# A two-layer graph attention kernel: a buffer of its own for the last products of W with a_dst, and the transposes of tile 4 ahead of two mask counts

## The chip, the cores and the metric

The kernel runs on one core of a Trainium2 chip. The core has five engines that work in parallel, each through its own queue in order: TensorE (PE; its weight loads are shown apart as PEld), VectorE (DVE), ScalarE (ACT), GpSimd (POOL) and SyncE (SP, which here only issues DMAs). The metric is the device time of one execution in microseconds; several executions are made, and their median is compared.

## The reference, cut to what matters

Two graph attention layers on 3327 nodes of 1024 features, each followed by a residual and a layer norm. The adjacency is an int32 matrix in which about one entry in 200 is set.

```python
def _L0_gnn_ref(x, adj, W, a_src, a_dst):        # H = 8 heads of 128
    h = (x @ W).reshape(C, H, D)
    h_heads = jnp.transpose(h, (1, 0, 2))
    alpha_src = jnp.einsum('hcd,hd->hc', h_heads, a_src)
    alpha_dst = jnp.einsum('hcd,hd->hc', h_heads, a_dst)
    e = alpha_src[:, :, None] + alpha_dst[:, None, :]
    e = jnp.where(e >= 0, e, NEG_SLOPE * e)
    e = jnp.where(adj[None] == 0, -jnp.inf, e)
    attn = jax.nn.softmax(e, axis=-1)
    out = jnp.einsum('hij,hjd->hid', attn, h_heads)
    return jnp.transpose(out, (1, 0, 2)).reshape(C, H * D)
...
x = _layernorm(x + _L0_gnn_ref(x, adj, L0_gnn_W, L0_gnn_a_src, L0_gnn_a_dst), axis=-1)
x = _layernorm(x + _L1_gnn_ref(x, adj, L1_gnn_W, L1_gnn_a1, L1_gnn_a2), axis=-1)
```

Layer 1 is the same with one head, its own W and vectors, and a ReLU on the result.

## The kernel before

The nodes are cut into NT = 26 tiles of 128 rows. There are three stages in time: the projection with the making of edge lists (to about 487 us of the span), the sparse sums of layer 0 (gathers of rows of h0_d), and those of layer 1 with its projection (gathers of rows of y_d). A dense arm stands behind a branch and isn't taken here. The change is in the first stage, where the order of the work on every engine is written out by hand: each engine does its part in the order in which the code names it.

What the first stage does for a tile t:

- `load_x(t)` brings the rows of x (tag "x", 3 buffers); `flip(t)` transposes them: 8 transposes on PE (L176) in two groups of four, each into a PSUM bank of tag "T" (2 buffers), and two copies on ACT (L179) into xT (3 buffers). The small matmuls of the counts use the tag "T" too.
- `project(t, c)` multiplies xT by the columns `CUTS0[c]` to `CUTS0[c+1]` of wt (L479, 8 steps; two records each in the trace) into an accumulator of tag "A" (2 buffers); `keep(t, c)` copies it out with ACT (L496, and for c = 2 L491 to L494) and, after the third, stores the tile.
- wt is W with 16 columns added at its right end: W times a_src and a_dst by heads. Chunk c = 2 holds them, so `project(t, 2)` needs them all.
- `score_column(k)` makes these columns for the k-th block of 128 rows of W. DVE multiplies by a_src out of PSUM (pr0, L579) and reduces (L580). For k < 6 POOL multiplies by a_dst (pr1, L576) and ACT sums it in eight pieces (L585). For k of 6 and 7 DVE does the second product too (L579 into pr1) and reduces it (L582). pr0 and pr1 have two buffers each.
- `count(t)` is the count of the mask's rows: POOL clears the diagonal (L308), ACT sums the 3328 bytes of each row (L311) and casts the sum (deg_b, L313), DVE packs the mask (L318); then `load_mask(t + 3)` issues the DMA of a later mask from POOL (L468).
- `Edges.ends` and `ends2` make running sums of the counts: a small matmul each (L327, L346), a copy on ACT (L328, L347), then small operations on POOL (L335 to L353). `factors` has four more on POOL (L296 to L299) behind ACT's L295.
- `listing()` is a generator of steps: DVE finds the set columns (`keys`, `columns`), `places` makes a matrix with ACT (L384, L385) and DVE (L391, L392), and PE sorts the lists with it (`give`: L411, L401), which ACT and DVE take out (`take`: L423 to L428, `sources`: L436 to L450). `pace()` calls the next steps after every second k of a paced `project`. The first call in `project(2, 2)` makes three steps: `count(3)`, `places` of tile 0, and the first `give`.

Between `score_column(7)` and `count(0)` the code makes constants of the lists with DVE and POOL by turns (`tri`, `edge_constants`, L615 to L630). DVE has these behind its last product.

Of the kernel before, what the change touches and what calls it, by code (L numbers as in the profile page):

```python
# [19 lines left out]
P = 128  # L20
# [6 lines left out]
def kernel(  # L27
# [29 lines left out]
    N, D = x.shape  # L57
# [76 lines left out]
    def load_rows(dst, src, t):  # L134

        n = rows(t)
        if n < P:
            nc.gpsimd.memset(dst, 0.0)
        for r in pieces(t):
            nc.sync.dma_start(dst[r], src[at(t, r), :])  # L140
# [312 lines left out]
    with ExitStack() as own, tc.manual_schedule():  # L453
        ph = Phase(own, "proj", {"A": 2, "S": 1, "T": 2})
# [4 lines left out]
        def load_x(t):  # L459
            if t < NT:  # L460
                xts[t] = ph.sbuf("x", [P, D], 3)
                load_rows(xts[t], x, t)

        def load_mask(t):
            if t < NT:
                ads[t] = masks[t % 4 if t < NT - 1 else 4]
                for r in pieces(t):
                    nc.gpsimd.dma_start(ads[t][r, :N], adj[at(t, r), :])  # L468

        def flip(t):  # L470
            xT[t] = ph.sbuf("xT", [P, KT, P], 3)
            for _ in ph.transposed(xT[t], xts.pop(t), (0, 1)):
                pass

        def project(t, c, paced=True):

            acc = accs[t, c] = bank("A", [P, CUTS0[c + 1] - CUTS0[c]], "mm")
            for k in range(KT):
                nc.tensor.matmul(  # L479
                    acc, xT[t][:, k, :], wt[:, k, CUTS0[c] : CUTS0[c + 1]], start=k == 0, stop=k == KT - 1  # L480
                )
                if paced and k % 2 == 1:
                    pace()
# [17 lines left out]
        def count(t):  # L501
            if t < NT:
                lists[t].words(ads.pop(t), junk)
                load_mask(t + 3)
# [63 lines left out]
        junk = pool.tile([P, NP], U8, bufs=1, name="junk")  # L568
        junk_h = pool.tile([P, DH], BF16, bufs=1, name="junk_h")
        def score_column(k):  # L570
            pr = [ph.sbuf(f"pr{n}", [P, D], 2) for n in range(2)]
            to = [wt[:, k, D + n * H : D + (n + 1) * H] for n in range(2)]
            heads = [pr[n].rearrange("p (h d) -> p h d", h=H) for n in range(2)]
            for n in range(2):
                if n and k < 6:
                    nc.gpsimd.tensor_tensor(pr[n], wt[:, k, :D], av, OP.mult)  # L576
                else:
                    a = avs[:, 2 * n : 2 * n + 2, :].rearrange("p a b -> p (a b)")
                    nc.vector.tensor_tensor(pr[n], wt[:, k, :D], a, OP.mult)  # L579
            nc.vector.tensor_reduce(to[0], heads[0], AX.X, OP.add)  # L580
            if k > 5:
                nc.vector.tensor_reduce(to[1], heads[1], AX.X, OP.add)  # L582
                return
            for h in range(H):
                nc.scalar.activation(junk_h, heads[1][:, h, :], AF.Copy, accum_out=to[1][:, h : h + 1])  # L585

        flip(0)
        score_column(0)
        score_column(1)
        load_mask(0)  # L590
        project(0, 0, False)
        keep(0, 0)
        flip(1)
        load_x(3)
        score_column(2)
        project(0, 1, False)
        keep(0, 1)
# [45 lines left out]
        keep(1, 2)  # L643
        lists[0].ends2(all_b)
        lists[1].ends(tri_b)
        count(2)
        flip(3)
        load_x(5)

        done[0], slots[:] = 4, [9, (NT - 3) * 12 + 13]  # L650
        project(2, 2)
        keep(2, 2)
        lists[1].ends2(all_b)
        lists[2].ends(tri_b)
        flip(4)
        project(3, 2)
        keep(3, 2)
        lists[2].ends2(all_b)
        for t in range(3, NT):
# [3 lines left out]
            if t == 12:  # L663
                n, own = NT - 1, pool.tile([P, NT], I32, bufs=1, name="own")
# [565 lines left out]
```

## Time and profile before

| what | value |
|---|---|
| median of 3 runs | 1908.4 us (1906.88 to 1909.48) |
| the profiled execution | 1904.2 us, span 1902.5 us |
| PE busy | 1502.7 us, 79% of the span |
| DVE busy | 1146.0 us, 60% |
| POOL busy | 1032.3 us, 54% |
| ACT busy | 546.5 us, 29% |
| mean granted TensorE clock | 0.914 |
| data moved by DMA | 567.76 MB, mean 298 GB/s |

The span is the time from the first to the last instruction of the profiled execution; 1.7 us of its time lie outside. A busy share is an average over stages that have different limits, so the table says little of the first 90 us; for these the profile has the timeline of each engine, with the idle time ahead of an instruction and what ended it, the list of who waited for whom, and the busy time by stretches. In such lines the engine comes first, then the line of the code, the operation, and the tile written and read. A wait for several semaphores is put down to the one that came last.

### The profile page before, as it was taken

What the parts mean: (1) busy time and instruction counts of PE and PEld (TensorE: products, weight loads), DVE (VectorE), ACT (ScalarE), POOL (GpSimd) and SP (SyncE); (2) the same over time, 40 slices, a digit from 0 to 9 for tenths busy, and PEclk for the clock granted to TensorE, in tenths of its full rate; (3) what the DMA queues carried; (4) which work ended last, traced back from release to release, by engine and by line L of the source; (5) the groups of instructions that cost most, each with busy time, mean ns of one, the idle gap of its engine ahead of it and who ended that gap; (6) DMA issues with size and microseconds to landing.
All of it is one profiled execution on the core that took longest, in us unless ns stands there. A gap on an engine that the chain in (4) does not pass through costs nothing.

```text
span 1902.5 us, 38082 instructions
## 1 busy us (share of the span) xinstructions
PE 1502.7 (79%) x14663; PEld 887.9 (47%) x14663; DVE 1146.0 (60%) x3058; ACT 546.5 (29%) x1422; POOL 1032.3 (54%) x1391
## 2 busy tenths in 40 slices
PE   8699999999366556555556555399999999999997
PEld 5355555566254545445445444144444444444443
DVE  5799999987286666666666666344444444444442
ACT  5554544452123222222222222012222212222220
POOL 3322222220477666676666764577766667666650
PEclk9899999999678788888888888699999999999999
DMA  7656555421799999999999997899999999999980
GB/s 182 88 115 131 111 104 106 87 72 39 276 369 400 400 401 399 376 406 398 390 388 392 398 383 279 325 401 407 403 370 385 380 378 373 354 372 373 365 326 33
DMA packets 171068, 567.76 MB, mean 298 GB/s; under 512 B 27690, under 2 KB 34346, under 8 KB 170878
## 3 DMA queue, kind: packets, MB, share of 16 engines
q0 software_dynamic: 131056, 455.68, 67.2%
q1 hardware_dynamic: 39822, 109.56, 15.3%
q8 instruction: 118, 1.93, 0.4%
q14 instruction: 72, 0.59, 0.1%
HBM read 578.85 MB, written 42.97 MB: 327 GB/s over the span
## 4 chain that ended last, share of the span: by engine, by line
PE 50%; DMA 24%; DVE 12%; ACT 6%; issue 4%; POOL 3%; DVEq 0%; ACTq 0%; SPq 0%; POOLq 0%
DMA src<-h_d,idx 22%; PE mm L1023 20%; PE acc L991 12%; PE mm L479 11%; DVE e L868 3%; ACT junk L311 3%; PE acc L896 2%; PE tr L176 2%; POOL src L801 2%; DVE pr L929 1%; ACT xT L179 1%; DMA wt<-in_L_gnn_W_dram 1%; PE acc L880 1%; DVE top L274 1%; PE xp L411 1%
## 5 line engine op out<-in xcount | busy, mean ns | idle before, releaser
L801 POOL DMA_INDIRECT src<-h_d,idx x416 | 443.3, 1066 | 201.6 <-PE acc L896 52.3
L801 POOL DMA_INDIRECT src<-y_d,idx x416 | 415.4, 999 | 222.1 <-PE acc L991 89.4
L896 PE MATMUL acc<-src,e 128*32 128x128 f32 x6656 | 267.7, 328 | 260.0 <-DVE e L868 259.6
L479 PE MATMUL mm<-wt,xT 128*128 128x347 f32 (+1 forms) x1248 | 402.5, 468 | 3.1 <-DMA wt<-in_L_gnn_W_dram 2.5
L1023 PE MATMUL mm<-wt,xT 128*128 128x512 f32 x832 | 383.3, 604 | 0.8 <-DVE o L1026 0.8
L896 PEld LDWEIGHTS acc<-src,e 128*32 128x32 f32 x6656 | 226.3, 133 | 316.7 <-DVE e L868 290.7
L479 PEld LDWEIGHTS mm<-wt,xT 128*128 128x128 f32 x1248 | 228.2, 192 | 111.2 <-ACT ht L496 6.7
L1023 PEld LDWEIGHTS mm<-wt,xT 128*128 128x128 f32 x832 | 152.2, 190 | 199.5 <-issue 179.1
L991 PE MATMUL acc<-src,es 128*32 128x342 f32 (+1 forms) x2496 | 205.6, 463 | 33.8 <-DVE es L982 30.9
L868 DVE TENSOR_TENSOR e<-oh,way 128x1024 f32<-128x1024 f32 x130 | 158.8, 1221 | 60.6 <-ACT w L866 60.3
L991 PEld LDWEIGHTS acc<-src,es 128*32 128x32 f32 x2496 | 71.5, 111 | 158.8 <-issue 113.1
L866 ACT ACTIVATE w<-way 128x32 f32<-128x32 f32 (+1 forms) x130 | 24.7, 190 | 399.7 <-DVE way L864 388.3
L1026 DVE SCALAR_TENSOR_TENSOR o<-mm,y 128x512 f32<-128x512 f32 x52 | 36.0, 692 | 166.1 <-PE mm L1023 166.1
L1005 ACT ACTIVATE z<-y,ri 128x342 f32<-128x342 f32 (+1 forms) x78 | 39.5, 569 | 313.8 <-DVE ri L1001 313.8
L863 DVE TENSOR_TENSOR way<-src,re 128x32 f32<-128x32 f32 x104 | 20.9, 201 | 171.6 <-DMA src<-h_d,idx 153.2
L179 ACT ACTIVATE xT<-tr 128x512 f32<-128x512 f32 x104 | 59.3, 595 | 150.7 <-PE tr L176 150.7
L979 DVE TENSOR_TENSOR way<-way,src 128x128 f32<-128x128 f32 x104 | 31.1, 299 | 89.9 <-DMA src<-y_d,idx 44.4
L311 ACT ACTIVATE junk<-ad 128x3328 uint8<-128x3328 uint8 x26 | 78.3, 3013 | 16.1 <-POOL ad L308 16.1
L848 ACT ACTIVATE own<-own,es 128x128 f32<-128x128 f32 x208 | 63.6, 388 | 59.7 <-DVE es L845 59.7
L880 PE MATMUL acc<-end,e 128*128 128x128 f32 x416 | 63.0, 313 | 15.3 <-DVE e L868 15.3
L335 POOL TENSOR_TENSOR place_of<-cnt 128x1 f32<-128x1 f32 x26 | 5.0, 191 | 122.1 <-ACT cnt L328 102.5
L296 POOL CAST mvs<-r 128x8 bf16<-128x8 f32 x26 | 6.0, 231 | 118.2 <-ACT r L295 118.2
(188 smaller groups left out, 1953.7 us busy)
## 6 DMA issues: line engine op xcount, KB each, us to landing
h_d<-ht SPq DMA_DIRECT2D x26, 520.0 KB
own<-h_d SPq DMA_DIRECT2D x26, 520.0 KB
y_d<-y SPq DMA_DIRECT2D x26, 514.0 KB
y<-y_d SPq DMA_DIRECT2D x26, 514.0 KB
x<-in_x_dram SPq DMA_DIRECT2D x25, 512.0 KB
y<-in_x_dram SPq DMA_DIRECT2D x25, 512.0 KB
out_dram<-o SPq DMA_DIRECT2D x25, 512.0 KB
ad<-in_adj_dram POOLq DMA_DIRECT2D x25, 415.9 KB
```

Of the source, the lines that this page charges most:

```text
L176: nc.tensor.transpose(tr[:, k, :], src[:, (4 * g + k) * P : (4 * g + k + 1) * P], ident)
L179: nc.scalar.activation(part, tr, AF.Copy)
L311: nc.scalar.activation(junk, ad, AF.Copy, accum_out=self.deg)
L479: nc.tensor.matmul(acc, xT[t][:, k, :], wt[:, k, CUTS0[c] : CUTS0[c + 1]], start=k == 0, stop=k == KT - 1)
L801: nc.gpsimd.indirect_dma_start(out=s[:, g, :w], out_offset=None, in_=table[:, :], in_offset=bass.IndirectOffsetOnAxis(ap=idx[:, t, b * NG ...
L848: nc.scalar.activation(hn, hn, AF.Copy, scale=es[:, n : n + 1])
L868: nc.vector.tensor_tensor(e, oh.unsqueeze(2).to_broadcast([P, ng, H, wide]), wp.unsqueeze(3).to_broadcast([P, ng, H, wide]), OP.mult,)
L880: nc.tensor.matmul(self.acc[h // 4][:, h % 4, :], e[:, 0, h, :], rowsof[:, 0, h, :], start=False, stop=h % 4 == 3,)
L896: nc.tensor.matmul(self.acc[h // 4][g * GT : (g + 1) * GT, h % 4, :], e[:, g, h, :], rowsof[:, g, h, :], start=first and h % 4 == 0, stop= ...
L991: nc.tensor.matmul(self.acc[c][to, :m], es[:, g, :], s[:, g, CUTS[c] : CUTS[c + 1]], start=b == 0, stop=b == EB,)
L1005: nc.scalar.activation(z[:, cut], self.res[:, cut], AF.Copy, scale=ri[:, 1:2])
L1023: nc.tensor.matmul(acc, xT[:, k, :], wt1[:, k, half], start=k == 0, stop=k == KT - 1)
```

## The change

The second product of DVE, for k of 6 and 7, goes into a tile of its own, pr2, with one buffer; pr1 is left to POOL and ACT. And `flip(4)` is named right behind `load_x(5)`, ahead of `count(2)`, which itself goes behind `flip(3)` and `load_x(5)`. Before, the order was `count(2)`, `flip(3)`, `load_x(5)`, and `flip(4)` came only after `project(2, 2)` with the counts that follow it.

```diff
         def score_column(k):
-            pr = [ph.sbuf(f"pr{n}", [P, D], 2) for n in range(2)]
+
+            tags = ("pr0", "pr1" if k < 6 else "pr2")
+            pr = [ph.sbuf(tag, [P, D], 1 if tag == "pr2" else 2) for tag in tags]
...
         keep(1, 2)
         lists[0].ends2(all_b)
         lists[1].ends(tri_b)
-        count(2)
         flip(3)
         load_x(5)
+        flip(4)
+        count(2)
 
         done[0], slots[:] = 4, [9, (NT - 3) * 12 + 13]
         project(2, 2)
         keep(2, 2)
         lists[1].ends2(all_b)
         lists[2].ends(tri_b)
-        flip(4)
         project(3, 2)
```

In the queues this means: on PE the 8 transposes of tile 4 stand behind those of tile 3, ahead of `project(2, 2)`; on ACT the four copies L179 of tiles 3 and 4 stand ahead of `count(2)`. The orders on DVE, POOL and SP are unchanged.

## The prediction

> **What bounds the kernel now.** I read the per-stage table first, then the list of waits of the first 450 us, then the timeline around those waits. The edited code lies in the first 90 us of the first stage. In the table each row has a stretch, its length, then busy us and instruction counts of PE, PEld, DVE, ACT and POOL, the granted clock, the DMA share and GB/s.
>
> ```profile
> 40.00:50.00 10.00, 10.00 (x35) 6.43 (x34) 8.22 (x14) 3.18 (x15) 2.26 (x11) 1.00 0.12 12
> 50.00:60.00 10.00, 4.77 (x15) 2.85 (x14) 8.21 (x50) 4.43 (x10) 2.88 (x19) 0.76 0.43 37
> 60.00:70.00 10.00, 7.45 (x28) 4.55 (x27) 7.49 (x22) 4.74 (x11) 5.54 (x26) 0.90 0.91 169
> 70.00:80.00 10.00, 1.82 (x15) 1.31 (x16) 4.63 (x14) 7.83 (x10) 0.94 (x3) 0.62 0.98 125
> 100.00:200.00 100.00, 96.99 (x672) 59.71 (x672) 91.67 (x259) 48.13 (x134) 26.11 (x122) 1.00 0.58 126
> ```
>
> From 100 us on PE (97%) and DVE (92%) are both full: whatever starts them sooner moves all that follows. Between 50 and 80 us PE is busy only 14 of 30 us, so time is to be had there. Who is waited for:
>
> ```profile
> PE xp L411 <- DVE place L391: 20.6, 15, 9.7
> DVE pr L579 <- ACT junk_h L585: 11.0, 1, 11.0
> PE op L327 <- ACT deg_b L313: 5.0, 1, 5.0
> ```
>
> These are total, times and longest. In order of time (start, duration, engine, line, operation, idle time before it in brackets):
>
> ```profile
> 38.51 1.22 DVE L579 TENSOR_TENSOR pr<-wt,avs 128x1024 f32<-128x1024 f32 x1 [11.02 <-ACT junk_h L585]
> ...
> 54.77 2.98 ACT L311 ACTIVATE junk<-ad 128x3328 uint8<-128x3328 uint8 x1 [10.52 <-POOL ad L308]
> ...
> 58.13 0.16 PE L327 MATMUL op<-deg_b,tri_b 128*128 128x1 bf16 x1 [5.05 <-ACT deg_b L313]
> 58.48 6.69 PE L479 MATMUL mm<-wt,xT 128*128 128x346 f32 x16 [0.19 <-ACT ht L496]
> ...
> 69.52 2.98 ACT L311 ACTIVATE junk<-ad 128x3328 uint8<-128x3328 uint8 x1 [3.31 <-POOL ad L308]
> ...
> 72.73 1.07 ACT L179 ACTIVATE xT<-tr 128x512 f32<-128x512 f32 x2
> 73.69 2.98 ACT L311 ACTIVATE junk<-ad 128x3328 uint8<-128x3328 uint8 x1
> 76.89 0.71 ACT L384 ACTIVATE away<-io_q,place_of 128x512 f32<-128x512 f32 x1
> ...
> 78.18 0.26 PE L411 MATMUL xp<-mvs,place 32*128 32x42 bf16 x12 [9.71 <-DVE place L391]
> ...
> 85.50 1.09 PE L176 MATMUL tr<-ident,x 128*128 128x128 f32 x8 [0.74 <-ACT cnt L328]
> ```
>
> So: DVE sits 11.02 us in front of the second product of k = 6, whose buffer ACT still reads for k = 4. Everything on DVE behind it (the edge constants) is late, so POOL's mask edit L308 and ACT's count L311 of tile 0 are late, and ACT's copy that frees PE's accumulator stands behind that count. Later ACT does count 2, two copies of flip 3, count 3, and only then L384, for which DVE and PE wait.
>
> [...] (L576 takes 2.35 to 2.39 us beside DVE work and without). [...] after 5.05 us idle, product (1,2) took 6.69 us, against 4.71 (18.84 us for 64 records, so for 16) in the run from 34.24.
>
> **Part 1, the buffer.** Instruction counts don't change; the wait of the product of k = 6 on ACT and POOL goes. That of k = 7 still waits for DVE's own reduction of k = 6, which is ahead in its queue: free. POOL and ACT keep pr1 for k up to 5. From 38.51 to the end of the last reduction at 46.50 is 7.99 us of unbroken DVE work. It now follows the product that starts at 26.28 and takes 1.2 us: 27.5 + 8.0 = 35.5, so 11.0 sooner. W and the vectors have landed (22.4).
>
> What is late next, by copying the old distances:
> - From 46.50 to L308's end takes 8.27 us, so L308 could end at 43.8. POOL's queue ahead of it (products to 35.2, the mask issue to 35.7) is clear; mask 0 landed long before (the DMA queues are empty at 32 to 35). ACT's copy at 43.79 lasts to 44.25: count 0 runs 44.3 to 47.5 with its deg_b.
> - ACT's copy of (2,1) then waits for PE (48.4), not PE for it. PE runs (0,2) to 53.1 as before and goes straight into (1,2), warm: 53.2 to 57.9.
> - Now (0,2) is the bound. ACT's L491 moves from 58.32 to 53.2, 5.12 sooner. From there L295, POOL's eleven small operations and L308 lead to count 1: 61.58 - 5.12 = 56.46. It ends with deg_b at 59.6. In the old run ACT then waited for PE ((1,2) ended at 65.17); now it need not, so L491 of tile 1 moves from 65.20 to 59.7: 5.5 sooner.
> - POOL's chain from there to L308 of mask 2 is unbroken (65.69 to 69.49), so count 2 moves from 69.52 to 64.0.
> Part 1 is 5.5 us.
>
> **Part 2, flip 4 ahead.** Nothing is added: 8 transposes and 2 ACT copies move. On PE they pass project (2,2) with its list steps and two count matmuls; on ACT the two copies of flip 4 go from behind counts 2 and 3, L384 and tile 2's copies to before count 2, and those of flip 3 pass count 2. SP's order is the same (load_x(5) stays behind the tile-1 store; x of tile 4 was issued at 24.22, its queue is quiet by 32). POOL's and DVE's orders are the same: masks 5 and 6 are issued 5.5 or more sooner.
> - Cost on ACT: copies of flip 3 start 0.7 after the transposes, which start at 66.21 - 5.5 = 60.7: 61.4 to 62.5. The two PSUM banks of tag T are freed in turn, so flip 4's transposes run at 62.0 and 62.6 and its copies end at 63.9. Count 2 cannot start before 64.0: the old 3.31 us of ACT idle hides all four. If PE is cold there (half clock), the copies end near 65.0 and cost up to 1.0. I take 0.1.
> - Gain: between counts 2 and 3 the copies leave ACT's way: 73.69 - 72.73 = 0.96. L384 moves by 5.5 + 0.96 - 0.1 = 6.4, and with it L391 and PE's L411 (78.18 to 71.8).
> - At the old place PE loses 0.74 of wait and about 0.93 to 1.1 of transposes: project (3,2) starts 86.43 - 84.59 = 1.84 sooner. Not all counts: ACT's count 4 at 91.51 could move 1.85, but POOL ends L308 of mask 4 at 89.86 in an unbroken chain from 84.98; so 1.6. DVE has 1.83 us idle in front of L391 at 96.34, so it follows.
> Part 2 is 0.86 + 1.6 = 2.5.
>
> Masks: 3 is issued at 43.8 instead of 54.68 into an empty DMA (mask 2 alone took 36 to 42), 4 at 56.4 instead of 61.49; needed at 64.3 and 83. [...]
>
> **Sum.** 5.5 + 2.5 = 8.0 us. After 96.9 the order on every engine is as before, so the rest shifts whole; in the gather stages the DMA is at 0.99 to 1.02 of its share and starts 8 sooner. The profiled execution took 1904.2 (span 1902.5): 1896.2. The median of the runs, 1908.4, lies 4.2 above that; I take the same difference off it: 1900.4. Bounds: 7.0 if flip 4 delays count 2, 8.3 if POOL is no brake at mask 4; runs spread by 2.6.
>
> **Rivals.**
> - Only the buffer pays: flip 4 runs cold, and the 1.84 at its old place is eaten by the ACT or POOL chain. For: POOL's chain there is unbroken. Gain 4.5 to 5.5, time 1903.4. Chance 0.12.
> - Part 1 is hidden, because something besides the buffer holds count 0 or count 1 (a mask landing late, or POOL's queue), and only part 2's 2.5 is left: 1905.9, which is no change within 0.2% (3.8 us, about what a measurement tells). Against: the DMA queues are empty at 32 to 35 us. Chance 0.09.
> - Slower: the granted TensorE clock of the later stages falls. Place: from about 1240 us to the end PE is 97% busy (97.25 of 100 in 1500 to 1600, clock 1.00). Price: 660 us by 0.97, 6.4 us for each per cent of clock; 1.25% eats the gain, 1.9% makes it slower by over 0.2%. For: the layer-0 stage already shows 0.75 to 0.84. Against: 1,100 us lie between, and the work there is the same. At 2.5% it costs 16: 1916. Chance 0.05.
> - The layout does not do what it says: the product of k = 6 still waits. The wait there is on the shared buffer alone, so I leave this within the second rival.
>
> **Numbers.** Forecast 0.74, rivals 0.12, 0.09, 0.05. Faster by over 0.2%: 0.74 + 0.12 = 0.86; same 0.09; slower 0.05. Both first cases with half the spread on each side give 1898.2 to 1904.8, which leaves out some 2 in 10.
>
> **What would show it.** L579's 11.02 wait gone and the last reduction near 35.5; count 0 near 44.3 and no 5.05 idle on PE at L327; count 1 near 56.5, count 2 near 64.0, four copies ahead of it by then; the wait before L411 still long, but ending near 71.8; the L411 of 96.88 at 88.8 or so; from there equal distances. I am wrong if count 2 starts well after POOL's L308, if a mask lands late, or if the end of the first stage (486 us) does not move by about 8.

## The result and the profile after

| | median of 4 runs | span of the profiled execution |
|---|---|---|
| before | 1907.64 us (1906.47 to 1909.48) | 1902.5 us |
| changed | 1901.98 us (1900.15 to 1903.19) | 1901.5 us |

The ratio is 0.9969, with a 95% interval of 0.9951 to 0.9986: 5.7 us off the median, with 2.7 to 9.3 inside the interval. The forecast was 8.0. The two profiled spans differ by 1.0 us only: the profiled execution of before (1904.2 us) was faster than all four of its timed runs, that of the changed kernel (1903.19) was the slowest of its four. So the profile of the changed kernel has to be read by where its time lies, not by its end.

From L571 on, line numbers of the changed kernel are two higher. Its timeline, from the views of DVE, ACT and PE (start, duration, engine, line, operation, idle time before in brackets):

```profile
34.15 1.21 DVE L584 TENSOR_REDUCE wt<-pr 128x8 f32<-128x1024 f32 x1
...
46.03 2.97 ACT L311 ACTIVATE junk<-ad 128x3328 uint8<-128x3328 uint8 x1
...
54.83 4.90 PE L479 MATMUL mm<-wt,xT 128*128 128x346 f32 x16
...
61.62 0.16 PE L327 MATMUL op<-deg_b,tri_b 128*128 128x1 bf16 x1 [1.89 <-ACT deg_b L313]
...
64.50 1.08 ACT L179 ACTIVATE xT<-tr 128x512 f32<-128x512 f32 x2 [0.26 <-PE tr L176]
65.77 2.98 ACT L311 ACTIVATE junk<-ad 128x3328 uint8<-128x3328 uint8 x1 [0.19 <-POOL ad L308]
...
68.98 2.96 ACT L311 ACTIVATE junk<-ad 128x3328 uint8<-128x3328 uint8 x1
...
72.17 0.71 ACT L384 ACTIVATE away<-io_q,place_of 128x512 f32<-128x512 f32 x1
...
73.46 0.27 PE L411 MATMUL xp<-mvs,place 32*128 32x42 bf16 x12 [7.34 <-DVE place L391]
```

The 11.02 us wait of DVE is gone, and its last reduction ends at 35.36 instead of 46.51. Count 0 no longer has 10.5 us of idle before it. PE goes from (0,2) into (1,2) without a gap and at full clock (granted 1.00 over these 4.90 us): before, the same product took 6.69 us at a mean granted clock of 0.73. Count 2 starts as soon as POOL lets it (0.19 us), with all four copies done ahead of it, and count 3 follows it directly. The list of waits of the first 450 us shows the same, with one wait that has grown (DVE's in front of `tri_b`, 0.40 us before):

```profile
PE xp L411 <- DVE place L391: 18.0, 14, 7.3
...
DVE tri_b L624 <- POOL tri L620: 1.9, 1, 1.9
PE op L327 <- ACT deg_b L313: 1.9, 1, 1.9
```

DVE is now early enough to wait for POOL's last product (k = 5, 34.70 to 37.08 us), which stands ahead of the constants in POOL's queue. The table by stretches (length; busy us and counts of PE, PEld, DVE, ACT, POOL; clock; DMA share; GB/s) has PE busy 9.7 of 10 us between 50 and 60, where it had 4.8:

```profile
20.00:30.00 10.00, 7.34 (x24) 4.94 (x25) 9.89 (x10) 5.94 (x25) 4.46 (x4) 0.83 0.91 146
...
50.00:60.00 10.00, 9.73 (x36) 6.14 (x35) 3.23 (x10) 3.12 (x8) 2.85 (x13) 1.00 0.33 69
```

The row from 20 to 30 shows what went against this run: a clock of 0.83 there, where the earlier profile had 1.00. W's last block, for which PE waits there, was hardly later (before, then changed):

```profile
22.46 0.85 PE L479 MATMUL mm<-wt,xT 128*128 128x347 f32 x2 [2.46 <-DMA wt<-in_L_gnn_W_dram]
22.66 0.85 PE L479 MATMUL mm<-wt,xT 128*128 128x347 f32 x2 [2.91 <-DMA wt<-in_L_gnn_W_dram]
```

But from 24.05 to 27.47 us PE had half clock in the changed kernel (granted 0.50) and full clock before (1.00): its next 32 records took 11.04 us, before 9.51. So ACT's copy of (2,0) starts at 45.67 instead of 43.79, and in what follows I count from that copy to the first gather (before, then changed):

```profile
43.79 0.46 ACT L496 ACTIVATE ht<-mm 128x347 f32<-128x347 f32 x1 [0.88 <-PE mm L479]
488.52 1.15 POOL L801 DMA_INDIRECT src<-h_d,idx  x1 [0.96 <-issue]
...
45.67 0.46 ACT L496 ACTIVATE ht<-mm 128x347 f32<-128x347 f32 x1 [0.88 <-PE mm L479]
482.35 1.15 POOL L803 DMA_INDIRECT src<-h_d,idx  x1 [0.96 <-issue]
```

In the table all but the first column are such distances; the two L384 are those of the place matrices of tiles 0 and 1.

| start, us | copy of (2,0) | count 1, after it | count 2 | L384 | second L384 | first gather |
|---|---|---|---|---|---|---|
| before | 43.79 | 17.79 | 25.73 | 33.10 | 51.78 | 444.73 |
| changed | 45.67 | 12.59 | 20.10 | 26.50 | 43.91 | 436.68 |

The first gather, where the first stage ends, is 8.05 us sooner by this count (6.17 on the clock: 488.52 and 482.35). The rest of the difference lies later: from the first gather to the first residual copy of layer 1 (L1005) it is 746.2 us before and 751.3 after, and from there to the end 667.7 and 667.8. Whether those 5 us of layer 0 belong to the change is one question for the experiments.

The count from this copy leaves something out: DVE's moved products run from about 27 to 35 us, ahead of it. The traces of all the experiments below tell whether they hold up PE there. From PE's first matmul on W's last block to the copy of (2,0) it is 21.33 us in the first profile of before, in which the granted clock is 1.00 all through this stretch; 22.88 to 23.01 in six profiles with one drop of 3.41 us (before again, the order alone, the changed kernel three times, the kernel with the pause); and 24.10 to 24.36 in three with a drop of 6.83 us (the buffer alone, both flips behind count 2, the place matrix ahead). So the distance goes with the clock. The three with the long drop all have pr2, but the second half of their drop begins at 25.5 to 26.1 us and DVE's moved product at 27.1 to 27.4, so this product can't be its cause.

### The profile page after: what moved, and what is told of

It is laid out like the page before. It is cut to its first block, busy times and chain, and to the rows that moved or that the text cites. A ratio compares the mean times of both kernels' runs of the same rounds, so it can differ in the third digit from the quotient of the medians.

```text
span 1901.5 us, 38079 instructions
## 1 busy us (share of the span) xinstructions
PE 1518.5 (80%) x14663; PEld 902.4 (47%) x14663; DVE 1146.6 (60%) x3058; ACT 546.6 (29%) x1422; POOL 1030.2 (54%) x1391
## 4 chain that ended last, share of the span: by engine, by line
PE 52%; DMA 24%; DVE 12%; ACT 6%; issue 4%; POOL 2%; SPq 0%; DVEq 0%; ACTq 0%; POOLq 0%
DMA src<-h_d,idx 20%; PE mm L1025 20%; PE acc L993 12%; PE mm L479 12%; DVE e L870 3%; PE acc L898 3%; ACT junk L311 3%; PE tr L176 2%; POOL src L803 2%; DMA src<-y_d,idx 2%; DVE pr L931 1%; PE acc L882 1%; DMA wt<-in_L_gnn_W_dram 1%; ACT xT L179 1%; PE xp L411 1%
## 5 line engine op out<-in xcount | busy, mean ns | idle before, releaser
L898 PE MATMUL acc<-src,e 128*32 128x128 f32 x6656 | 278.5, 337 | 253.6 <-DVE e L870 253.5
L898 PEld LDWEIGHTS acc<-src,e 128*32 128x32 f32 x6656 | 234.8, 137 | 311.3 <-DVE e L870 284.3
L179 ACT ACTIVATE xT<-tr 128x512 f32<-128x512 f32 x104 | 59.4, 596 | 151.0 <-PE tr L176 150.9
L882 PE MATMUL acc<-end,e 128*128 128x128 f32 x416 | 67.7, 328 | 13.3 <-DVE e L870 13.3
```

The costliest lines, as they stand in the source:

```text
L179: nc.scalar.activation(part, tr, AF.Copy)
L882: nc.tensor.matmul(self.acc[h // 4][:, h % 4, :], e[:, 0, h, :], rowsof[:, 0, h, :], start=False, stop=h % 4 == 3,)
L898: nc.tensor.matmul(self.acc[h // 4][g * GT : (g + 1) * GT, h % 4, :], e[:, g, h, :], rowsof[:, g, h, :], start=first and h % 4 == 0, stop= ...
```

## The experiments

The kernel before takes 1906.5 us in one group of runs (chip 8 in the record), 1989.4 and 1966.3 in the other two (both chip 5), so levels differ between groups even on one chip. Each time is compared with the kernel before in its own group. The ratios are those of the record, with 95% intervals; they aren't the quotients of the two medians beside them and can differ from these by about 0.1%.

### The changed kernel, each part alone, and the parts of part 2

The changed kernel again, unedited:

> The changed kernel once more, for its profile and for the spread. Times inside the first stage are told from the start of ACT's first copy L496, which marks the landing of W. Theory A (both parts lie on the path and the shift of the first stage passes whole to the end; the 2.3 us that the medians lack are scatter of single executions): the first gather starts 8.0 us sooner than before when counted from that copy, and the median of five rounds is 6 to 8 us below before. Theory B (layer 0 gives a part back, with a lower granted clock, whenever the first stage ends sooner): the first gather 8.0 sooner, the median only 4 to 6 below, and the layer-0 stage longer than before by 2 to 4 us.

Measured: 1980.62 against 1989.39, ratio 0.9957 (0.9940 to 0.9974), 8.8 us less. First gather 436.86 after the copy of (2,0), 7.87 sooner than before.

The expectations of this group count from another mark, ACT's first L496. From there it is 458.98 us here and 465.17 before: 6.2 sooner, not 8.0. The three kernels below would come to 3.4, 1.4 and 2.7 by that mark. I left it after these runs, because PE's drop to half clock, shown above, lies behind it and differs in length from one execution to another; all that follows counts from the copy of (2,0).

Layer 0 took 820.9 us here. This group has no profile of the kernel before, and the three other profiles of the group gave 809.9 to 816.8, so this says nothing for or against theory B.

The buffer alone:

```diff
-            pr = [ph.sbuf(f"pr{n}", [P, D], 2) for n in range(2)]
+
+            tags = ("pr0", "pr1" if k < 6 else "pr2")
+            pr = [ph.sbuf(tag, [P, D], 1 if tag == "pr2" else 2) for tag in tags]
...
         count(2)
         flip(3)
         load_x(5)
...
         flip(4)
         project(3, 2)
```

> The buffer pr2 alone, with the old order of flips and counts. Theory A: the last reduction of DVE ends 11 us sooner, count 1 5.1 and count 2 5.5 us sooner, L384 and the first gather 5.5 us sooner (from the first L496); time 5.5 below before. Rival (count 0 or count 1 is held by something besides the buffer, and the gain of the changed kernel comes from the order): first gather less than 3 us sooner.

Measured: counted from the copy, count 1 at 12.59 (5.2 sooner), count 2 at 20.09 (5.6), L384 at 27.46 (5.6), first gather 438.97 (486.60 on the clock, copy at 47.63), 5.76 sooner. Time 1983.40 against 1989.39, ratio 0.9982 (0.9964 to 1.0000), an interval that reaches no change.

The order alone:

```diff
-        count(2)
         flip(3)
         load_x(5)
+        flip(4)
+        count(2)
...
-        flip(4)
         project(3, 2)
```

> The order alone, with pr1 shared as before. Theory A: count 2 starts where it did, L384 1.0 sooner, the first gather 2.5 us sooner (0.9 from the copies that no longer part counts 2 and 3, 1.6 from the transposes that no longer stand ahead of project (3,2)); time 2.5 below before. Rival (the order pays only once the buffer has made room, or is eaten by POOL's chain at mask 4): less than 1 us.

Measured: count 2 at 25.61, L384 at 32.01 (1.1 sooner), first gather 442.40 (488.86, copy at 46.46), 2.33 sooner. Time 1986.02, ratio 0.9978 (0.9960 to 0.9996). The two parts give 5.76 + 2.33 = 8.09 at the first gather, and together they gave 8.05 and 7.87: they add up. Whole times can't part them, with intervals of 7 us in this group; the traces can, with one profile of each kernel.

Flip 4 moved, but both flips behind count 2:

```diff
+        count(2)
         flip(3)
         load_x(5)
         flip(4)
-        count(2)
```

> The changed kernel, but with flip(4) behind flip(3) and both behind count(2), so that ACT's four copies stand between counts 2 and 3. It tells apart the two halves of part 2. Theory A: L384 moves only 5.5 - 1.1 = 4.4 us against before (four copies between the counts instead of two), the gain of 1.6 at the old place of the transposes stays, so the first gather is 6.0 sooner, 2.0 later than in the changed kernel. Rival (the place of the copies on ACT doesn't matter, since PE or POOL decides): 8.0 sooner as in the changed kernel.

Measured: first gather 439.94, 4.8 sooner than before and 3.3 later than in the changed kernel; L384 at 29.64, 3.5 sooner than before. Time 1983.75, ratio 0.9970 (0.9954 to 0.9987). The place on ACT matters, by more than I expected (4.4 for L384, 6.0 for the first gather). The timeline of this kernel, from the views of ACT and PE:

```profile
70.63 1.06 ACT L179 ACTIVATE xT<-tr 128x512 f32<-128x512 f32 x2
72.41 0.60 ACT L179 ACTIVATE xT<-tr 128x512 f32<-128x512 f32 x1 [0.72 <-PE tr L176]
73.27 0.60 ACT L179 ACTIVATE xT<-tr 128x512 f32<-128x512 f32 x1 [0.26 <-PE tr L176]
73.76 2.97 ACT L311 ACTIVATE junk<-ad 128x3328 uint8<-128x3328 uint8 x1
...
71.26 1.97 PE L176 MATMUL tr<-ident,x 128*128 128x128 f32 x8 [6.06 <-ACT xT L179]
```

Flip 3 fills both PSUM banks of tag T and waits for its copies behind count 2. Flip 4's transposes can start only then, after 6.06 us of idle; they take 1.97 us, where they took 1.15 in the changed kernel, and ACT waits 0.72 and 0.26 for them. From deg_b of count 2 (70.52) to count 3 are 3.2 us, where the changed kernel has 0.1 (68.87 to 68.98). In the changed kernel the same four copies fall into ACT's wait for POOL and cost nothing.

### Does a shift of the first stage pass to the end?

A pause put back at the end of the first stage, whose result is overwritten:

```diff
         big = ph.sbuf("big", [P, NT, 2], 1)
+        for _ in range(7):
+            nc.vector.tensor_reduce(big[:, 0, :1], wt[:, 0, :D], AX.X, OP.add)
```

> The changed kernel with seven more DVE reductions of a 128x1024 block at the end of the first stage, ahead of the flag on which all engines wait: by the trace 1.13 us each, 7.9 us in a row, which nothing hides. Their result is overwritten. Theory A (a shift of the first stage's end passes whole to the end): first gather 7.9 us later than in the changed kernel, the time back at that of before within 2 us. Theory B (layer 0 gives a part back when it starts sooner): the time only 4 to 6 us above the changed kernel's.

The timeline of DVE in this kernel:

```profile
477.91 8.74 DVE L691 TENSOR_REDUCE big<-wt 128x1 f32<-128x1024 f32 x7
```

The pause took 8.74 us, not 7.9: these seven reductions come 1.25 us apart, where those of `score_column` come 1.13 apart. They all write one place and have another shape; which of the two counts wasn't tried. The first gather comes at 445.39 after the copy, 8.71 later than in the changed kernel. Time 1906.05 against 1906.47, ratio 1.0004 (0.9996 to 1.0012): this kernel lies between 0.8 us below and 2.3 above before, so the pause costs what the change gains, to within about 2 us.

The kernel before, once more in the same group:

> The kernel before once more, for a second profile. Theory A: counted from ACT's copy of (2,0), which ends what stands ahead of the changed part, the first gather comes at 444.7 us as in the first profile, within 0.3; the start of that copy and the length of layer 0 scatter by several us without any change. Theory B: layer 0 is shorter than in the profile of the changed kernel on the same chip by 2 us or more.

Measured: ratio 0.9999 (0.9991 to 1.0007); first gather 444.43 after the copy, but that copy at 46.13, later than in the first profile and than in the changed kernel. Layer 0 took 743.4 us here, 745.9 with the pause, 744.1 and 746.9 in the two kernels below that ran on the same chip. The timeline of PE shows where the late copy comes from:

```profile
23.25 1.53 PE L479 MATMUL mm<-wt,xT 128*128 128x347 f32 x2 [3.29 <-DMA wt<-in_L_gnn_W_dram]
24.57 1.91 PE L176 MATMUL tr<-ident,x 128*128 128x128 f32 x8
```

In the first profile the same wait was 2.46 us, the two records took 0.85 and the transposes 1.04. So this scatter belongs to the kernel before as well. Its first gather differs by 0.30 us from that of the first profile, counted from the copy; the gains above are counted from the first.

The changed kernel a third time, in another group:

> The changed kernel once more, beside a kernel before on the same chip in five rounds. Theory A: 7 to 9 us below before; the 5.7 of the four first runs was scatter of where W lands and of layer 0. Theory B: 5 to 6.5 below again.

Measured: 1958.54 against 1966.27, ratio 0.9963 (0.9944 to 0.9981), 7.7 us less; first gather 436.68. Theory B would have layer 0 longer whenever the first stage ends sooner. On the chip of the group with the pause it took 746.9, 744.1, 745.9 and 743.4 us after stages that ended at 478.4, 482.1, 490.2 and 490.6: no order of the size that theory B needs. The 5.1 us by which the first pair of profiles differs is more than these four spread, and stays unexplained. Against theory B speak the pause and the two medians of 8.8 and 7.7 below before, though a give-back of 1 to 2 us can't be excluded.

### What is late next

The place matrix of tile 0 ahead of counts 2 and 3:

```diff
+                if not old:
+                    new.places()
+                    yield
                 count(t + 4)
                 yield
...
-                if new:
+                if new and old:
                     new.places()
...
         flip(4)
+        next(steps)
         count(2)
 
-        done[0], slots[:] = 4, [9, (NT - 3) * 12 + 13]
+        done[0], slots[:] = 5, [9, (NT - 3) * 12 + 13]
```

> The changed kernel with the place matrix of tile 0 (L384, L385, L391, L392) ahead of count 2 and count 3, since what it needs is known by then. Theory A (what is late next is ACT's two counts ahead of L384): PE's first list matmul comes 6 us sooner than in the changed kernel, then PE waits for deg_b of count 3 at the running sum of tile 3; the first gather 3.2 us sooner, time 3 below the changed kernel, 11 below before. Rival: DVE, at 92% the fuller engine from 100 us on, takes over and less than 1 us is left.

Measured: 1896.29 against 1906.47, ratio 0.9950 (0.9936 to 0.9963), 10.2 less than before. First gather 434.78: 1.9 sooner than in the changed kernel, not 3.2. The timeline of PE:

```profile
68.45 0.24 PE L411 MATMUL xp<-mvs,place 32*128 32x42 bf16 x12 [0.66 <-DVE place L391]
...
74.60 0.16 PE L327 MATMUL op<-deg_b,tri_b 128*128 128x1 bf16 x1 [4.39 <-ACT deg_b L313]
74.63 4.96 PE L479 MATMUL mm<-wt,xT 128*128 128x346 f32 x8
```

The 7.34 us wait is down to 0.66, and PE then waits 4.39 for count 3, as expected. What was missed is PE's pace after that idle time: the next eight records take 4.96 us, where they took 3.64 in the changed kernel, and these 1.3 us are about what the first gather lacks of the 3.2. DVE did not take over.

The DMA of mask 0 issued later:

```diff
-        load_mask(0)
         project(0, 0, False)
...
         score_column(2)
+        load_mask(0)
         project(0, 1, False)
```

> The changed kernel with the DMA of mask 0 issued one POOL product later (near 20.3 instead of 14.3 us), behind most of W. Theory A (W lands late and by chance because mask 0's transfer runs beside it, and the 3 us wait also costs PE its clock): PE's wait for the last block of W goes from 2.9 us to under 1, the copy of (2,0) starts 2 to 4 us sooner, and as much is gained at the first gather; mask 0 is still there at 44. Rival (W's own transfers and x set the landing): no change of that copy beyond its scatter.

Measured: 1893.46 against 1906.47, ratio 0.9940 (0.9926 to 0.9953), 13.0 less than before. The copy of (2,0) starts at 40.76; in the ten other profiles above it started between 43.79 and 47.63. Its timeline of PE:

```profile
13.40 6.88 PE L479 MATMUL mm<-wt,xT 128*128 128x347 f32 x16
...
21.00 9.51 PE L479 MATMUL mm<-wt,xT 128*128 128x347 f32 x32
...
57.54 3.68 PE L176 MATMUL tr<-ident,x 128*128 128x128 f32 x16 [0.68 <-ACT cnt L328]
```

The 16 records of (0,0) run through in 6.88 us (a weight load waits 0.6 us for W, no matmul does), and the next 32 in 9.51, as in the first profile of before; with a late W they took 11.04 in the changed kernel. In the ten others PE's matmuls waited 2.46 to 3.31 us for W's last block. The DMA views of 18 to 20 us fit theory A: before, the queue of POOL's DMAs, where mask 0 is, fills 81.4% and SP's, with W, 25.5%; here SP's fills 95.1% and POOL's has no traffic. Mask 0 is there in time. PE is now so early that count 0 waits for DVE's and POOL's constants (2.63 us after the copy instead of 0.36), but count 1 is at 12.59, as in the changed kernel. The first gather is 437.67 after the copy, 1.0 more than in the changed kernel: flips 3 and 4 took 3.68 us here, nearly all of it at a granted clock of 0.50.

Both of these edits in one kernel:

> The changed kernel with both of the last two edits: mask 0's DMA one POOL product later, and the place matrix of tile 0 ahead of counts 2 and 3. Theory A: the gains add up, since one lies ahead of the copy of (2,0) and the other behind: first gather near 476.5 us, time 15 below before. Rival (with PE's products sooner, POOL or DVE holds count 0 and the second gain goes): 13 below, as with the mask alone.

Measured: the first gather at 476.37 us, and 434.50 after a copy at 41.87; time 1953.01 against 1966.27, ratio 0.9933 (0.9911 to 0.9954), 13.3 less. At the first gather both gains are there, though count 0 came 1.90 us after the copy; no matmul waited more than 0.43 us for W. The interval of the time is too wide to tell this kernel from the one with the mask alone. Its median is 5.5 us below that of the changed kernel in the same group; the kernel with the mask alone had no changed kernel beside it, and the interval of its ratio overlaps those of the changed kernel.

## Why the prediction was right

- **The buffer.** The last reduction was put at 35.5 and ended at 35.36. That PE's (0,2) becomes the bound, and count 1 follows it by the old distance, was put at 12.7 after the copy of (2,0) (56.46 - 43.79) and came at 12.59. Part 1 was 5.5 and measured 5.76 by itself.
- **Count 2.** 64.0 was 20.2 after the copy; measured 20.10. The four copies were hidden by ACT's wait for POOL, as worked out, with 0.19 us to spare. The slower flips, priced at up to 1.0, did come in other executions: in the kernel with the later mask (3.68 us for the sixteen transposes) count 2 came at 21.00, and in the one with the pause, where ACT waits 0.56 and 0.26 us for the transposes of flip 4, at 20.48. That the changed kernel was spared in its three profiles is luck.
- **Part 2.** 2.5 forecast, 2.33 measured alone. The two halves, 0.86 and 1.6, stand at the two L384: in the kernel with the order alone the first is 1.09 sooner and the second 2.34, so that the halves are 1.1 and 1.25. In that kernel eight records of PE between the two took 3.62 us, where before they took 3.23: these 0.39 us are about what the second half lacks. The cap by POOL's chain isn't shown: count 4 starts at 91.88, and POOL's L308 of mask 4 (91.84) and ACT's own work ahead of it (91.85) end together.
- **The sum.** 8.0 forecast for the end of the first stage; 8.05, 7.87 and 8.05 in three profiles (0.3 less against the second profile of before). The whole time fell by 5.7, 8.8 and 7.7 in three groups, and the pause of 8.74 us brought it back to before. The first result alone didn't tell this from the first rival: 1901.98 lies between the forecast's 1900.4 and the rival's 1903.4, nearer to the latter. The range of 1898.2 to 1904.8 doesn't come out of its own terms either: half of 2.6 on each side gives 1899.1 to 1904.7, and the result lies in both.
- **What was mis-sized** is the scatter: "runs spread by 2.6" came from three runs, and the 25 runs of before in the group with the pause spread by 8.1 (1901.45 to 1909.56). The landing of W and PE's clock behind it move all that follows by up to 4 us from one execution to the next (the copy of (2,0) at 43.79 to 47.63), and the profile of before that I counted from had a granted clock of 1.00 there. That is why the profiled spans show only 1.0: the traces place the difference in PE's clock behind W (1.7 us, with 0.2 for W itself) and in the length of layer 0 (5.1 us). What sets the latter from one execution to the next stays open. Only one of the first four runs has a profile, so where their 5.7 came from isn't shown; its interval of 2.7 to 9.3 holds the 8.0.
- **The rivals.** Only the buffer pays: refuted by the order alone and by the sum. Part 1 hidden: refuted by the trace of the buffer alone (5.76; its whole time alone wouldn't do). A lower clock in later stages: from the first residual copy of layer 1 to the end it was 667.7 and 667.8 us, so not there.

## What to carry to other kernels

A buffer that two slow readers share can hold up an engine whose own work is early: look at who reads the buffer's other half, and price the gain by the next bound (here PE's product), not by the wait that goes (11 us gone, 5.8 gained). The copies out of PSUM were free here while ACT waited for POOL anyway (0.19 us were left of that wait), and cost more than their own time behind count 2, an instruction of 2.98 us: the banks that they should free stopped PE for 6.06 us, and its next transposes took 1.97 us in place of 1.15. So ask of a copy what its engine does at that place, and who waits for the bank. Where the spans of two single executions differ by less than their scatter, count from a mark near the edit to a mark just behind the stage, choose the mark before the runs, and say what of the edit lies ahead of it.

## What the runs showed that I had not expected

In these runs the clock of PE after a gap is not given by the gap alone. In the changed kernel flips 3 and 4 follow gaps of 1.89 and 0.68 us and their first eight transposes take 1.09 us; in the kernel with the later mask the same two gaps stand there, and sixteen take 3.68 with a gap of 0.23 us among their weight loads. From about 17 to 119 us of all twelve traces the granted clock changes only at marks that are multiples of 3.41 us apart, and the marks lie elsewhere in each execution (half clock from 24.05 to 27.47 and from 68.43 to 78.67 in the changed kernel, from 55.25 to 62.08 and from 72.32 to 82.56 in the first profile of before). The table by stretches, cut at these marks, for the later mask and then for the changed kernel (the column behind the length is PE's busy time, the third from the end the clock):

```profile
54.23:57.64 3.41, 0.85 (x6) 0.33 (x5) 3.17 (x13) 3.26 (x10) 0.46 (x3) 1.00 0.93 76
57.64:61.05 3.41, 3.41 (x16) 3.04 (x17) 1.94 (x7) 1.79 (x3) 2.88 (x16) 0.50 0.98 220
...
58.19:61.60 3.41, 1.54 (x7) 0.88 (x6) 3.13 (x11) 3.31 (x4) 0.61 (x2) 1.00 0.62 48
61.60:65.01 3.41, 2.46 (x18) 1.97 (x18) 2.63 (x8) 2.44 (x11) 2.45 (x14) 1.00 0.99 163
```

With the later mask both gaps fall into one such window of 3.41 us, in which PE is busy for only 0.85 us, and the next window is at half clock. In the changed kernel a mark parts them, PE is busy for 1.54 us of the window, and the clock stays. All 348 such windows of the twelve traces fall apart in this way. At full clock, PE was busy for at most 1.47 us in each of the 27 that were followed by half clock, and for at least 1.52 in the 268 that were not. At half clock, it was busy for at least 3.22 us in the 27 that were followed by full clock, and for at most 2.78 in the 26 that were not. So in these traces the next clock went with PE's busy time within one such window. The prediction had its slower product behind one gap of 5.05 us; here about 1.9 us of idle within one window (3.41 - 1.47) were enough.
